# Expert weights of two routed layers: a load from DRAM per tile, or one resident copy in SBUF that each tile copies from

## The chip, the cores and the metric

The kernel runs on one core of a Trainium2 chip. The metric is the device time of one execution in microseconds. Thirteen executions of the kernel before have a median of 928.32 us, between 923.73 and 933.23.

## The reference

Four residual layers work on x of 16 batches x 128 tokens x 128 features, all fp32, each on the layer norm of x:

```python
x = x + xcond(layernorm(x), cond, ctx)      # self- and cross-attention, GLU
x = x + moe0(layernorm(x))                  # a shared expert and 7 routed ones
x = x + slots(cond, ctx, layernorm(x))      # 3 turns of slot attention
x = x + moe1(layernorm(x))                  # 8 routed experts

def moe0(x):                                # hidden width 352
    scores, idx = top_k(softmax(x @ wr.T + rb), 2)
    w = scores / scores.sum()
    out = expert(x, sg, su, sd)             # silu(x @ g.T) * (x @ u.T) @ d
    for e in range(7):
        out = out + w[e] * expert(x, rg[e], ru[e], rd[e])
    return out

def moe1(x):                                # hidden width 512
    probs = softmax(x @ w_gate + b_gate)
    e, p = argmax(probs), max(probs)
    return p * (relu(x @ W1[e] + b1[e]) @ W2[e] + b2[e])
```

A token goes to two of seven experts in the first routed layer and to one of eight in the second. Which ones is known only on the chip.

## The kernel before, in words

All tokens stay in SBUF in one tile, r (128 partitions x 16 batches x 128). The kernel goes through attention, the GLU (to some 495 us), the first routed layer, the slot attention and the second routed layer in that order, in groups of four batches.

A routed layer is an object of class `Routed`: m0 with two experts a token (nk = 2), m1 with one (nk = 1). Its work has four steps.

- **Routing.** Each group's normed rows go to DRAM (`rows`, the tensor tok, by SyncE's queue), with the token's weight beside them. DVE marks each token's experts.
- **Sorting** (`sort`). Every expert's tokens fill tiles of 128 rows; an expert's last tile may be partly empty. The number of tiles is a constant, the largest that can occur: (4096 + 7 x 127) // 128 = 38 for m0 and (2048 + 8 x 127) // 128 = 23 for m1. The sort, mostly small DVE operations, leaves for each tile the rows to fetch (frm), the rows to write (to), and in `row` the place of its expert's weights.
- **Tiles** (`tiles`). Each tile's 128 rows are fetched by an indirect DMA on POOL (L874, zs), transposed on TensorE and copied by ScalarE (L886, L888, zT). For m0, `moe0_up` (L978) makes two up-projections of 384 columns each into PSUM (gum). `silu_gate` makes th on ScalarE (L953), gs and a on VectorE (L955, L956). `moe0_down` (L989) projects back to 128 features (ynm) and ScalarE scales by the token's weight wk (L987, L993). An indirect DMA on POOL (L895) writes the rows to res in DRAM. For m1, `moe1_up` (L1231) makes two halves of the 512 hidden columns (h1n), with the relu on ScalarE (L1236) and VectorE (L1238). `moe1_down` (L1246) projects back, VectorE adds the bias and scales (L1248, L1249, ysn), and the rows go to the output.
- **Combine** (`combine`). For m0 the rows of res are read back per group (L925, ygm, eight loads on SyncE's queue) and added to r on TensorE (L921, L926) and ScalarE (L927). The slot attention's first turn waits for its group.

The loop over tiles is pipelined by its order of statements: the first half of tile j's up-projection, then the transpose of tile j + 1, then the second half, then the down-projection of tile j - 1 (`finish`), which also issues the weights of a later tile and the fetch of a later tile.

**Weights.** A tile's weights (gate, up and down side by side, 1152 columns for m0, 1156 with the biases for m1) come from DRAM by one DMA on SyncE's queue (L864). Its address is a register that SyncE loads from `row` (L861). Six buffers of 1156 columns let five loads go ahead of the tile at work. Only the first two are issued before the fetches: the later ones read their rows from `row_late`, a copy of `row` that is made to depend on the last steps of the sort.

**What sets the order.** Within an engine, instructions run in the order in which they are listed; a scheduler in the framework may move an instruction ahead of others while the kernel is built, except in a stretch marked as manual. Buffers of one tag in a pool come free in order, and a writer waits until the last reader of the old contents is done. So slot work that doesn't depend on the routed layer (`slot_prologue`, `slot_context`, L1031 to L1077) can stand between tiles or behind them, as the scheduler decides.

Of the kernel before, what the change touches and what calls it, by code (L numbers as in the profile page):

```python
# [11 lines left out]
F32 = mybir.dt.float32  # L12
BF16 = mybir.dt.bfloat16
I32 = mybir.dt.int32
# [17 lines left out]
WBUFS = 6  # L32
WT = 1156
# [24 lines left out]
def pixart_kernel(  # L58
# [577 lines left out]
    def wide(nm):  # L636
# [3 lines left out]
    wt = ctx.enter_context(tc.tile_pool(name="wt", bufs=WBUFS))  # L640
# [4 lines left out]
    cb = slp.tile([P, B, D], F32, name="cb")  # L645
    dma(
        out=cb,
        in_=rows[0, R_COND * D : (R_COND + B) * D].partition_broadcast(P).rearrange("p (b d) -> p b d", d=D),
    )


    def glu_body(g, hT):
        u = ph.tile([P, 4, 512], F32, name=f"u{g}", tag="act")
        for c in range(4):
            ps = {}
            for j in (1, 0):
                ps[j] = wide(f"glu{g}_{c}_{j}")
                PE.matmul(ps[j], lhsT=gluw[:, 4 * j + c, :], rhs=hT, start=True, stop=True)
            ge = ph.tile([P, 512], F32, name=f"ge{g}_{c}", tag="gate")
            S.activation(ge, ps[1], AF.Gelu, bias=col(C_FFB1 + 4 + c))  # L660
            V.scalar_tensor_tensor(u[:, c, :], ps[0], col(C_FFB1 + c), ge, ALU.add, ALU.mult)
        y = psX.tile([P, 4, D], F32, name=f"yg{g}", tag="x")
        token_major(y, lambda c: u[:, c, :], lambda c: gluw[:, 8 + c, :], 4)
        rg = r[:, 4 * g : 4 * g + 4, :]
        V.tensor_tensor(rg, y, rg, ALU.add)
# [38 lines left out]
    w_issue = []  # L704

# [5 lines left out]
    class Routed:  # L711


        def __init__(self, nm, ne, nk, w, w0, tok):
            self.nm, self.ne, self.nk, self.w, self.w0, self.tok = nm, ne, nk, w, w0, tok
            self.ws, self.zs, self.st = [], {}, {}
            self.b0, self.nb = 0, B
            nb = self.nb
            self.nt = n_tiles(nk * nb * P, ne)
            self.oh = self.tile([P, nk, nb, ne], "oh")  # L720
            self.any = self.tile([P, nb + 1, ne], "any")
            self.cum = self.tile([P, nb + 1, ne], "cum")
            V.memset(self.any[:, nb, :], 0.0)
            V.memset(self.cum[:, 0, :], 0.0)
# [32 lines left out]
        def sort(self):  # L757
# [27 lines left out]
            V.tensor_scalar(te, te, float(ne - 1), float(P), ALU.min, ALU.mult)  # L785
            V.tensor_scalar(self.row, te, float(self.w0), None, ALU.add)
# [52 lines left out]
            self.row_late = self.tile([1, nt], "row_late", I32)  # L839
            self.ahead = nk * (FETCH - 1)  # L840
            for _ in range(2):
                self.weights()
            for j in range(self.ahead):
                self.fetch(j)
            late = self.frm[:1] if nk == 2 else self.zs[0][:1, :nt].bitcast(I32)
            V.scalar_tensor_tensor(self.row_late, late, 0, self.row, ALU.mult, ALU.add)
            for _ in range(2, WBUFS - 1):
                self.weights()
# [5 lines left out]

        def weights(self):
            j = len(self.ws)
            if j == self.nt:
                return
            w = wt.tile([P, WT], F32, name=f"w{self.nm}{j}", tag="w")
            with tc.issue_after(w_issue[-1]) if w_issue else ExitStack():  # L860
                row = nc.sync.value_load(  # L861
                    (self.row if j < 2 else self.row_late)[0:1, j : j + 1], min_val=self.w0, max_val=self.w0 + (self.ne - 1) * P
                )
                w_issue.append(dma(out=w[:, : self.w.shape[1]], in_=self.w[bass.ds(row, P), :]).ins)  # L864
            self.ws.append(w)
# [13 lines left out]
        def tiles(self, up, down):  # L879

            nt, zs, zT, acts = self.nt, self.zs, {}, {}
            dst = res0 if self.nk == 2 else out.rearrange("b s d -> (b s) d")
            wrote = dram_disjoint_views(dst, nt)

            def turn(j, t):
                PE.transpose(t, zs[j][:, :D], ident)  # L886
                zT[j] = ph.tile([P, P], F32, name=f"zTn{self.nm}{j}", tag="zTn", bufs=3)
                S.copy(zT[j], t)  # L888

            def finish(j):  # L890
                y = ys4[:, 1 + j % 3, :]
                ys = ph.tile([P, D], F32, name=f"ys{self.nm}{j}", tag="ysn", bufs=6)
                down(self.ws[j], acts[j], y, ys, self, j)
                self.weights()
                G.indirect_dma_start(  # L895
                    out=wrote[j], out_offset=bass.IndirectOffsetOnAxis(ap=self.to[:, j : j + 1], axis=0),
                    in_=ys, in_offset=None, **({} if self.nk == 2 else dict(bounds_check=NTOK - 1, oob_is_err=False)),
                )
                self.fetch(j + self.ahead)


            ys4 = psX.tile([P, 4, D], F32, name=f"yn{self.nm}", tag="x")
            turn(0, ys4[:, 0, :])
            for j in range(nt + 1):
                steps = up(self.ws[j], zT[j], f"{self.nm}{j}") if j < nt else None
                if steps:
                    spare = next(steps)
                if j + 1 < nt:
                    turn(j + 1, spare)
                if steps:  # L910
                    acts[j] = next(steps)
                if j >= 1:
                    finish(j - 1)
# [44 lines left out]
    def moe0_shared(R, i, zT):  # L958
        g = R.b0 // 4 + i
        a = ph.tile([P, 3, 512], F32, name=f"ma{g}", tag="act")  # L960
        for c in range(3):
# [4 lines left out]
            silu_gate(a[:, c, :], ps[0], ps[1], f"s{g}_{c}", 512)  # L966
        y = psX.tile([P, 4, D], F32, name=f"ym{g}", tag="x")
        token_major(y, lambda c: a[:, c, :], lambda c: wsh[:, 2 * IP + c * D : 2 * IP + (c + 1) * D], 3)
# [48 lines left out]
    def work(g, nm, shape=(P, 512)):  # L1017

        return spool.tile(list(shape), F32, name=nm, tag=f"w{g}")

# [30 lines left out]
    def slot_prologue():  # L1051
        G.memset(vu[:, :, D : D + 1], 1.0)
        G.tensor_tensor(cb[:1], cb[:1], brow[:1, R_B2S, :].unsqueeze(1).to_broadcast([1, B, D]), ALU.add)
# [105 lines left out]
    def slot_mlp(it, g, hT):  # L1159
# [11 lines left out]
            yf, lhsT=ones[:1, :], rhs=cb[:1, 4 * g : 4 * g + 4, :].rearrange("p a d -> p (a d)"), start=True, stop=False  # L1171
# [52 lines left out]
    def moe1_up(w, zT, nm):  # L1224
        acts = []
        for j in range(2):
# [6 lines left out]
            for c in range(2):  # L1233
                src, b1 = ps[:, c * P : (c + 1) * P], 2 * M1 + 2 * j + c
# [9 lines left out]
    def moe1_down(w, a, y, ys, R, j):  # L1244
        for c in range(4):
            PE.matmul(y, lhsT=a[c], rhs=w[:, M1 + c * D : M1 + (c + 1) * D], start=(c == 0), stop=(c == 3))  # L1246
        z = R.zs[j]
        V.tensor_tensor(ys, y, w[:, 2 * M1 + 4 : 2 * M1 + 4 + D], ALU.add)  # L1248
        V.scalar_tensor_tensor(ys, ys, z[:, D : D + 1], z[:, D + 1 :], ALU.mult, ALU.add)  # L1249


    spool = ctx.enter_context(tc.tile_pool(name="sp", bufs=2))
# [36 lines left out]
    m1 = Routed("n", EX1, 1, moe1_w, 0, tok1)  # L1289
    zT = {}  # L1290
# [8 lines left out]
    m0.tiles(moe0_up, moe0_down)  # L1299
    slot_prologue()  # L1300
# [11 lines left out]
def _layout(a):  # L1312
# [33 lines left out]
    def wide(w):  # L1346
# [5 lines left out]
        cat([w1, chunks(w2), b1.reshape(-1, P).T, np.broadcast_to(b2, (P, D))], axis=1)  # L1352
# [38 lines left out]
```

## Time and profile before

| | |
|---|---|
| median of 13 executions | 928.32 us |
| profiled execution, its own time | 931.63 us |
| span of its trace | 929.7 us |
| mean granted TensorE clock | 0.945 |
| busy: TensorE, VectorE, ScalarE, POOL | 89%, 64%, 48%, 37% |
| moved by DMA | 61.82 MB |
| first up-projection of m0's tiles, last down-projection's end | 543.8, 648.2 us |
| first up-projection of m1's tiles, last down-projection's end | 850.1, 925.1 us |

A line of the groups names the source line, the engine, the operation, output and inputs by the program's names (buffer numbers left out), the shapes and the count, then busy us and the mean ns of one, then the idle time just before and what ended it. A line of the timeline gives start and duration in us, then engine, line, operation and count, and in brackets the idle time before it. A releaser is inferred from semaphore events. Names end in m for the first routed layer and in n for the second.

### The profile page before, as it was taken

The page shows a single profiled execution, that of the slowest core. Times are in us where ns is not written, and L with a number is a line of the kernel's source. Part 1 is how long each engine was busy: PE and PEld are TensorE (multiplying, and loading weights), DVE is VectorE, ACT ScalarE, POOL GpSimd, SP SyncE. Part 2 cuts the span into 40 slices and gives each one's busy share as a digit, 9 for nine tenths or more (in the row PEclk, how much of TensorE's full clock was granted, in tenths as well). Part 3 has the DMA queues.
Part 4 walks back from the last instruction along what each step waited for, and adds up shares of the span by engine and source line. Part 5 has one row for each costly group of instructions (what it writes and reads, how often), then busy time and mean ns, then how long its engine had stood idle before and what let it go on. Part 6 is the DMA issues. An engine that isn't in the chain of part 4 may idle for free.

```text
span 929.7 us, 16297 instructions
## 1 busy us (share of the span) xinstructions
PE 827.2 (89%) x5847; PEld 654.8 (70%) x5847; DVE 592.4 (64%) x1845; ACT 442.0 (48%) x950; POOL 346.5 (37%) x408
## 2 busy tenths in 40 slices
PE   6999999998999999999999788789858979967786
PEld 5688888877777877777665477779446756646675
DVE  4587776669566666668778634445477758764333
ACT  3666667665554444444222022334477677831222
POOL 2333333234232213224420446654433334423554
PEclk9999999999999999999999779999979979975989
DMA  8100000000000000002001437775300000026773
GB/s 323 54 2 1 1 2 2 1 1 1 2 1 1 2 1 2 1 2 73 1 23 48 154 94 240 244 244 186 91 1 1 1 1 1 24 49 219 232 228 107
DMA packets 29563, 61.82 MB, mean 66 GB/s; under 512 B 4266, under 2 KB 18045, under 8 KB 28843
## 3 DMA queue, kind: packets, MB, share of 16 engines
q1 hardware_dynamic: 25211, 51.70, 17.4%
q0 software_dynamic: 4272, 9.09, 3.2%
q8 instruction: 46, 0.75, 0.3%
q14 instruction: 34, 0.28, 0.1%
HBM read 54.01 MB, written 7.23 MB: 66 GB/s over the span
## 4 chain that ended last, share of the span: by engine, by line
PE 64%; DVE 19%; POOL 5%; ACT 4%; issue 3%; DMA 2%; another core or an unknown queue 2%; SPq 0%; POOLq 0%; ACTq 0%; DVEq 0%
PE gum L978 6%; PE po L441 6%; PE pv L339 6%; PE te L431 5%; PE ya L451 5%; PE s L380 4%; PE pk L332 3%; PE ynm L989 3%; PE pq L322 3%; PE s L389 3%; PE ynn L1246 3%; PE h1n L1231 2%; DVE ri L412 2%; DVE e L405 1%
## 5 line engine op out<-in xcount | busy, mean ns | idle before, releaser
L416 POOL TENSOR_TENSOR e<-e,ri 128x1024 f32<-128x1024 f32 (+1 forms) x64 | 100.6, 1573 | 250.8 <-DVE ri L413 207.3
L400 DVE TENSOR_REDUCE mx<-s 128x8 f32<-128x1024 f32 (+1 forms) x64 | 64.5, 1007 | 48.5 <-PE s L389 39.6
L412 DVE TENSOR_REDUCE ri<-e 128x8 f32<-128x1024 f32 (+1 forms) x64 | 64.2, 1003 | 27.2 <-ACT e L408 26.2
L432 ACT COPY eT<-te 128x512 f32<-128x512 f32 (+1 forms) x96 | 56.4, 587 | 51.0 <-PE te L431 50.4
L978 PE MATMUL gum<-zTnm,wm 128*128 128x128 f32 x456 | 65.5, 286 | 11.1 <-ACT zTnm L888 8.5
L431 PEld LDWEIGHTS te<-ident,e 128*128 128x128 f32 (+1 forms) x512 | 61.5, 144 | 19.6 <-issue 11.5
L431 PE MATMUL te<-ident,e 128*128 128x128 f32 (+1 forms) x512 | 74.8, 274 | 0.0
L322 PE MATMUL pq<-ha,wa 128*128 128x256 f32 x256 | 66.9, 398 | 3.8 <-DVE r L455 2.8
L441 PE MATMUL po<-eT,v 128*64 128x128 f32 (+1 forms) x1024 | 69.4, 277 | 0.0
L978 PEld LDWEIGHTS gum<-zTnm,wm 128*128 128x128 f32 x456 | 59.2, 199 | 13.6 <-ACT zTnm L888 9.7
L408 ACT ACTIVATE e<-e 128x1024 f32<-128x1024 f32 (+1 forms) x64 | 57.1, 892 | 23.1 <-DVE e L405 21.4
L441 PEld LDWEIGHTS po<-eT,v 128*64 128x64 f32 (+1 forms) x1024 | 58.0, 137 | 11.8 <-DVE eT L432 6.3
L405 DVE TENSOR_TENSOR e<-s,mx 128x1024 f32<-128x1024 f32 (+1 forms) x64 | 63.8, 997 | 2.0
L451 PEld LDWEIGHTS ya<-wa,oT 128*128 128x128 f32 x512 | 60.8, 192 | 3.9 <-issue 1.4
L451 PE MATMUL ya<-wa,oT 128*128 128x128 f32 x512 | 62.6, 275 | 0.0
L322 PEld LDWEIGHTS pq<-ha,wa 128*128 128x128 f32 x256 | 46.5, 198 | 12.2 <-DVE r L455 4.2
L874 POOL DMA_INDIRECT zsm<-tok,frmm x38 | 36.7, 967 | 43.7 <-DVE secm L852 21.6
L895 POOL DMA_INDIRECT res<-ysm,tom x38 | 37.3, 982 | 31.5 <-ACT ysm L993 18.2
L343 ACT COPY v<-pv 128x512 f32<-128x512 f32 (+1 forms) x64 | 37.3, 585 | 22.9 <-PE pv L339 22.9
L445 ACT COPY oT<-po 128x512 f32<-128x512 f32 x47 | 27.1, 576 | 42.8 <-PE po L441 42.8
L955 DVE SCALAR_TENSOR_TENSOR gsm<-thm,gum 128x384 f32<-128x384 f32 x38 | 21.1, 554 | 37.6 <-ACT thm L953 17.9
L380 PE MATMUL s<-k,ha 128*128 128x308 f32 x128 | 42.6, 436 | 0.0
(388 smaller groups left out, 1889.2 us busy)
## 6 DMA issues: line engine op xcount, KB each, us to landing
wm<-in_moe_w_dram SPq DMA_DIRECT2D x38, 576.0 KB
wn<-in_moe_w_dram SPq DMA_DIRECT2D x23, 578.0 KB
wa<-in_attn_w_dram SPq DMA_DIRECT2D x4, 1024.0 KB
ygm<-res SPq DMA_DIRECT2D x8, 256.0 KB
tok<-stm SPq DMA_DIRECT2D x4, 258.0 KB
tok<-stn SPq DMA_DIRECT2D x4, 258.0 KB
x<-in_x_dram SPq DMA_DIRECT2D x8, 128.0 KB
cb<-in_rows_dram SPq DMA_DIRECT2D x1, 1024.0 KB
```

The lines of the kernel that those rows point to most:

```text
L322: PE.matmul(pq[:, j, :], lhsT=wqk[:, w : w + P], rhs=hT, start=True, stop=True)
L380: PE.matmul(ps[:, par, : 4 * nk].rearrange("p (j k) -> p j k", k=nk), lhsT=st["qT"][:, i * P : (i + 1) * P], rhs=st["kT"][:, h0 : h0 + 4, ...
L400: V.tensor_reduce(self.mx, self.ps, AX.X, ALU.max)
L405: V.tensor_tensor(self.e, self.ps, self.mx.unsqueeze(3).to_broadcast([P, 2, 4, nk]), ALU.subtract)
L408: S.activation(self.e, self.e, AF.Exp, scale=1.0 / math.sqrt(DH))
L412: V.tensor_reduce(self.ri, self.e, AX.X, ALU.add)
L416: G.tensor_tensor(self.e, self.e, self.ri.unsqueeze(3).to_broadcast([P, 2, 4, self.nk]), ALU.mult)
L431: PE.transpose(t[:nk, j, :], e[:, par, j, :], ident)
L432: (copies or (S.copy, V.tensor_copy))[par](eT[:nk, par], t[:nk])
L441: PE.matmul(po[par * DH : (par + 1) * DH, j, :], lhsT=st["v"][:nk, i, 8 * hg + 2 * j + par, :], rhs=eT[:nk, par, j, :], start=True, stop=True,
L451: PE.matmul(y, lhsT=oT[:, c, :], rhs=st["wo"][:, 1024 + c * D : 1024 + (c + 1) * D], start=(c == 0), stop=(c == 7),)
L978: PE.matmul(ps[j][:, c * P : (c + 1) * P], lhsT=w[:, k : k + P], rhs=zT, start=True, stop=True)
```

## The change

The weights of all experts of a layer lie in SBUF in one tile, `wall`. It is loaded once per layer by `load()`, with one DMA for each expert on SyncE's queue (7 x 576 KB for m0, 8 x 578 KB for m1). m0's load is issued ahead of the GLU and the routing. m1's load goes into the same buffer, is issued behind m0's tiles and ahead of the slot attention, and so waits until the last tile of m0 has copied its weights.

Each tile still has its own weight tile, now three buffers instead of six. It is filled by two copies out of `wall`: the up part by VectorE (768 columns for m0, 644 for m1 with its biases) and the down part by ScalarE (384 and 512). Each of the two engines loads the address into a register of its own. Two tiles' copies are made in the sort, the others in `finish`. `row` now holds a column of `wall` and not a row of DRAM; `row_late` is gone.

The loop over tiles stands in a stretch of manual schedule, so that its instructions keep the order in which the kernel states them.

Room in SBUF is made in three places: the intermediate tiles of the GLU and of the shared expert take four tags of work tiles that the slot attention also uses; the work tiles move into the pool ph, and their old pool is gone; and the tile cb of condition rows, 16 rows wide on 128 partitions, becomes four rows wide with four groups of 32 partitions. m1's weights are laid out with the biases ahead of the second matrix.

The diff, cut to its core:

```diff
-WBUFS = 6
-WT = 1156
+WBUFS = 3
+UP0, DN0 = 768, 384
+UP1, DN1 = 644, 512
...
-    wt = ctx.enter_context(tc.tile_pool(name="wt", bufs=WBUFS))
+    wt = ctx.enter_context(tc.tile_pool(name="wt", bufs=1))
...
-    cb = slp.tile([P, B, D], F32, name="cb")
-    dma(
-        out=cb,
-        in_=rows[0, R_COND * D : (R_COND + B) * D].partition_broadcast(P).rearrange("p (b d) -> p b d", d=D),
-    )
-
+    cb = slp.tile([P, 4, D], F32, name="cb")
+    for g in range(4):
+        k = (R_COND + 4 * g) * D
+        dma(
+            out=cb[32 * g : 32 * g + 32],
+            in_=rows[0, k : k + 4 * D].partition_broadcast(32).rearrange("p (b d) -> p b d", d=D),
+        )
...
+    def work(g, nm, shape=(P, 512)):
+
+        return ph.tile(list(shape), F32, name=nm, tag=f"w{g}")
...
-        u = ph.tile([P, 4, 512], F32, name=f"u{g}", tag="act")
+        u = [work(c, f"u{g}_{c}") for c in range(4)]
...
-            self.nm, self.ne, self.nk, self.w, self.w0, self.tok = nm, ne, nk, w, w0, tok
-            self.ws, self.zs, self.st = [], {}, {}
+            self.nm, self.ne, self.nk, self.tok = nm, ne, nk, tok
+            self.zs, self.st, self.ws = {}, {}, []
+            self.up, self.dn = (UP0, DN0) if nk == 2 else (UP1, DN1)
+            self.w, self.w0, self.wn = w, w0, self.up + self.dn
...
-            V.tensor_scalar(te, te, float(ne - 1), float(P), ALU.min, ALU.mult)
-            V.tensor_scalar(self.row, te, float(self.w0), None, ALU.add)
+            V.tensor_scalar(self.row, te, float(ne - 1), float(self.wn), ALU.min, ALU.mult)
...
-            self.row_late = self.tile([1, nt], "row_late", I32)
             self.ahead = nk * (FETCH - 1)
-            for _ in range(2):
-                self.weights()
             for j in range(self.ahead):
                 self.fetch(j)
-            late = self.frm[:1] if nk == 2 else self.zs[0][:1, :nt].bitcast(I32)
-            V.scalar_tensor_tensor(self.row_late, late, 0, self.row, ALU.mult, ALU.add)
-            for _ in range(2, WBUFS - 1):
+            for _ in range(WBUFS - 1):
                 self.weights()
...
+        def load(self):
+
+            self.wall = wt.tile([P, EX1 * (UP1 + DN1)], F32, name=f"wall{self.nm}", tag="wall")
+            for e in range(self.ne):
+                dma(
+                    out=self.wall[:, e * self.wn : (e + 1) * self.wn],
+                    in_=self.w[self.w0 + e * P : self.w0 + (e + 1) * P, :],
+                )
+
         def weights(self):
+
             j = len(self.ws)
             if j == self.nt:
                 return
-            w = wt.tile([P, WT], F32, name=f"w{self.nm}{j}", tag="w")
-            with tc.issue_after(w_issue[-1]) if w_issue else ExitStack():
-                row = nc.sync.value_load(
-                    (self.row if j < 2 else self.row_late)[0:1, j : j + 1], min_val=self.w0, max_val=self.w0 + (self.ne - 1) * P
-                )
-                w_issue.append(dma(out=w[:, : self.w.shape[1]], in_=self.w[bass.ds(row, P), :]).ins)
+            w = wt.tile([P, UP1 + DN1], F32, name=f"w{self.nm}{j}", tag="w", bufs=WBUFS)
+            for eng, k, n, copy in ((V, 0, self.up, V.tensor_copy), (S, self.up, self.dn, S.copy)):
+                at = eng.value_load(self.row[0:1, j : j + 1], min_val=0, max_val=(self.ne - 1) * self.wn)
+                copy(w[:, k : k + n], self.wall[:, bass.ds(at + k, n)])
             self.ws.append(w)
...
-            ys4 = psX.tile([P, 4, D], F32, name=f"yn{self.nm}", tag="x")
-            turn(0, ys4[:, 0, :])
-            for j in range(nt + 1):
-                steps = up(self.ws[j], zT[j], f"{self.nm}{j}") if j < nt else None
-                if steps:
-                    spare = next(steps)
-                if j + 1 < nt:
-                    turn(j + 1, spare)
-                if steps:
-                    acts[j] = next(steps)
-                if j >= 1:
-                    finish(j - 1)
+            with tc.manual_schedule():
+                ys4 = psX.tile([P, 4, D], F32, name=f"yn{self.nm}", tag="x")
+                turn(0, ys4[:, 0, :])
+                for j in range(nt + 1):
+                    steps = up(self.ws[j], zT[j], f"{self.nm}{j}") if j < nt else None
+                    if steps:
+                        spare = next(steps)
+                    if j + 1 < nt:
+                        turn(j + 1, spare)
+                    if steps:
+                        acts[j] = next(steps)
+                    if j >= 1:
+                        finish(j - 1)
...
-        a = ph.tile([P, 3, 512], F32, name=f"ma{g}", tag="act")
+        a = [work(c, f"ma{g}_{c}") for c in range(3)]
...
-        G.tensor_tensor(cb[:1], cb[:1], brow[:1, R_B2S, :].unsqueeze(1).to_broadcast([1, B, D]), ALU.add)
+        row_add(cb, R_B2S, 4)
...
-            PE.matmul(y, lhsT=a[c], rhs=w[:, M1 + c * D : M1 + (c + 1) * D], start=(c == 0), stop=(c == 3))
+            PE.matmul(y, lhsT=a[c], rhs=w[:, UP1 + c * D : UP1 + (c + 1) * D], start=(c == 0), stop=(c == 3))
         z = R.zs[j]
-        V.tensor_tensor(ys, y, w[:, 2 * M1 + 4 : 2 * M1 + 4 + D], ALU.add)
+        V.tensor_tensor(ys, y, w[:, M1 + 4 : M1 + 4 + D], ALU.add)
...
-    spool = ctx.enter_context(tc.tile_pool(name="sp", bufs=2))
...
     m1 = Routed("n", EX1, 1, moe1_w, 0, tok1)
+    m0.load()
     zT = {}
...
     m0.tiles(moe0_up, moe0_down)
+    m1.load()
     slot_prologue()
```

More of the change, by code (lines that the diff above doesn't have):

```diff
@@ L660, in glu_body @@
             S.activation(ge, ps[1], AF.Gelu, bias=col(C_FFB1 + 4 + c))
-            V.scalar_tensor_tensor(u[:, c, :], ps[0], col(C_FFB1 + c), ge, ALU.add, ALU.mult)
+            V.scalar_tensor_tensor(u[c], ps[0], col(C_FFB1 + c), ge, ALU.add, ALU.mult)
         y = psX.tile([P, 4, D], F32, name=f"yg{g}", tag="x")
-        token_major(y, lambda c: u[:, c, :], lambda c: gluw[:, 8 + c, :], 4)
+        token_major(y, lambda c: u[c], lambda c: gluw[:, 8 + c, :], 4)
         rg = r[:, 4 * g : 4 * g + 4, :]
@@ L702, in pixart_kernel @@
     G.iota(jt, pattern=[[1, NTM]], base=0, channel_multiplier=0, allow_small_or_imprecise_dtypes=True)
-    w_issue = []
     batch_row = rt.tile([P, 2 * B], F32, name="batch_row")
@@ L965, in moe0_shared @@
                 PE.matmul(ps[j], lhsT=wsh[:, w : w + P], rhs=zT, start=True, stop=True)
-            silu_gate(a[:, c, :], ps[0], ps[1], f"s{g}_{c}", 512)
+            silu_gate(a[c], ps[0], ps[1], f"s{g}_{c}", 512)
         y = psX.tile([P, 4, D], F32, name=f"ym{g}", tag="x")
-        token_major(y, lambda c: a[:, c, :], lambda c: wsh[:, 2 * IP + c * D : 2 * IP + (c + 1) * D], 3)
+        token_major(y, lambda c: a[c], lambda c: wsh[:, 2 * IP + c * D : 2 * IP + (c + 1) * D], 3)
         rg = r[:, 4 * g : 4 * g + 4, :]
@@ L1015, in pixart_kernel @@
     vu0 = slp.tile([NC, D], F32, name="vu0")
-    def work(g, nm, shape=(P, 512)):
-        return spool.tile(list(shape), F32, name=nm, tag=f"w{g}")
     def slot_context(g):
@@ L1170, in slot_mlp @@
         PE.matmul(
-            yf, lhsT=ones[:1, :], rhs=cb[:1, 4 * g : 4 * g + 4, :].rearrange("p a d -> p (a d)"), start=True, stop=False
+            yf, lhsT=ones[32 * g : 32 * g + 1, :], rhs=cb[32 * g : 32 * g + 1].rearrange("p a d -> p (a d)"),
+            start=True, stop=False,
         )
@@ L1233, in moe1_up @@
             for c in range(2):
-                src, b1 = ps[:, c * P : (c + 1) * P], 2 * M1 + 2 * j + c
+                src, b1 = ps[:, c * P : (c + 1) * P], M1 + 2 * j + c
                 if j == 0:
@@ L1351, in _layout @@
     moe1 = [
-        cat([w1, chunks(w2), b1.reshape(-1, P).T, np.broadcast_to(b2, (P, D))], axis=1)
+        cat([w1, b1.reshape(-1, P).T, np.broadcast_to(b2, (P, D)), chunks(w2)], axis=1)
         for w1, w2, b1, b2 in zip(*[a["L1_ffn_" + n] for n in ("W1", "W2", "b1", "b2")])
```

## The prediction

> **What bounds the kernel now.** I read the counts, then the 40 slices (TensorE is busy nearly everywhere, the DMA engines only at the start and in two later stretches), then the chain of waits, then a table of windows over the two late stretches. Those are the two loops over routed tiles, the only place where the change touches much. The first loop (m0, 38 tiles) runs from its first up-projection at 543.8 us to its last down-projection at 648.2: 104.4 us, 2.75 us a tile. The second (m1, 23 tiles) runs from 850.1 to 925.1: 75 us, 3.26 us a tile. The windows give span, then busy time of PE, weight load, DVE, ACT and POOL, granted clock, DMA share and GB/s:
>
> ```profile
> 580.00:600.00 20.00, 14.89 (x119) 13.58 (x117) 8.03 (x18) 5.82 (x18) 12.72 (x13) 1.00 0.79 240
> 620.00:640.00 20.00, 20.00 (x180) 20.00 (x180) 12.40 (x30) 9.76 (x29) 9.31 (x10) 1.00 0.90 289
> 880.00:900.00 20.00, 13.88 (x90) 12.71 (x91) 6.72 (x22) 4.45 (x15) 11.04 (x12) 0.88 0.74 228
> ```
>
> The second row is the loop with nothing in its way: 180 matmuls in 20 us at full clock, 19 passes a tile, so 2.12 us. The first row is the same loop with its fetches and weight loads: PE idles a quarter of the time. The loads are these:
>
> ```profile
> wm<-in_moe_w_dram SPq DMA_DIRECT2D x38, 576.0 KB
> wn<-in_moe_w_dram SPq DMA_DIRECT2D x23, 578.0 KB
> ```
>
> So m0 loses 104.4 - 38 x 2.12 = 24 us to waits. Part is POOL: one row fetch (967 ns) and one row write (982 ns) a tile start 1.25 us apart when nothing else waits, 2.5 us a tile while both go on (26 of 38 tiles). Part is the traffic: the chain has several pieces of 2.5 us in these stages put down to "another core or an unknown queue", and one of 6.62 us at 535.6, ahead of the first tile.
>
> **What the change removes.** All 61 tile loads from DRAM (35 MB), with them their share in those unknown waits. The most that this can give m0 is the 24 us, and only if nothing slower stands in the loop.
>
> **What it adds to m0's loop.** The order of instructions in the changed kernel shows DVE's list of tile j as: gs(j), a(j), wk(j-1), a register load, then the copy of the 768 up columns of w(j+1). Two buffers of three are filled ahead, so tile j's step copies the weights that tile j+1's first matmul, next on PE after ynm(j-1), needs. That copy stands behind a(j), and a(j) behind both of tile j's up-projections. In the kernel before, a load ran several tiles ahead and no engine copied. So a new loop closes: gum(j), th(j), gs(j), a(j), wk, copy w(j+1), gum(j+1). Its pieces are in an iteration of before that started after a stall:
>
> ```profile
> 588.36 0.94 PE L978 MATMUL gum<-zTnm,wm 128*128 128x128 f32 x6 [1.18 <-ACT zTnm L888]
> ...
> 589.44 0.27 ACT L888 COPY zTnm<-gum 128x128 f32<-128x128 f32 x1 [0.48 <-issue]
> ...
> 589.61 0.50 ACT L953 ACTIVATE thm<-gum 128x384 f32<-128x384 f32 x1
> 589.87 0.27 DVE L987 TENSOR_SCALAR wk<-zsm,sgnm,secm 128x1 f32<-128x1 f32 x1
> ...
> 590.13 0.56 DVE L955 SCALAR_TENSOR_TENSOR gsm<-thm,gum 128x384 f32<-128x384 f32 x1
> ...
> 590.79 0.56 DVE L956 SCALAR_TENSOR_TENSOR am<-gsm,gum 128x384 f32<-128x384 f32 x1
> ```
>
> From gum's first matmul to th 1.25 (the next tile's transpose and its ACT copy go ahead of th, in both kernels), to gs 1.77, to a 2.43, a's end 2.99, plus wk 0.27: 3.26 us before the copy can start. The transfer of the instruction's result to PE costs some 0.05 (in these rows one engine starts 0.02 to 0.05 after the other's end).
>
> The copy itself: before has no DVE copy inside SBUF. Ends: not under 0.34, the 77x128 TENSOR_SCALAR of zc (336 ns), a sixth of the elements; not over 1.00, the 128x1024 reduction of e (L412, 1003 ns mean over both its sizes). I take 0.55, the duration of the loop's own DVE operations on 384 columns with two operands, since a copy has one operand and no PSUM in it. Period: 3.26 + 0.55 + 0.05 = 3.86 us, between 3.65 and 4.31. 38 tiles: 146.7 us, against 104.4: **+42 us** (+34 to +59). Of the old limits, PE (2.12) and POOL (2.5) fit under this period, so none of their waits is added; that is also why the removed traffic returns nothing here.
>
> The ACT copy (384 down columns, 0.5 by the 128x384 th row) stands behind ys(j-1), which ends some 2.6 us into the tile. It ends near 3.1 and is needed only by ynm(j+1): nothing. Cover gone, it would cost only what exceeds 3.8.
>
> The register load is unpriced. On SP, the load (270 ns median) and its register operations (152) take 0.65 us from the load's start to the DMA's issue (at 568.18), with SP otherwise idle. On DVE it has no operand of the loop, so the sequencer may do it while a(j) is still at work: 0 to 0.65 a tile, 0 to 25 us in m0, and the same step in m1 0 to 15. I take 0, as the back-to-back DVE rows start without a gap (gs to a: 0.66 with 0.56 busy), so dispatch runs ahead; the other end is a rival below.
>
> The Trainium skill, "VectorE: DVE Perf Modes", section "Mode 2×_2P — use both read ports for one tensor", has a one-source fp32 operation within SBUF at two elements a cycle. An estimate from its 0.96 GHz and its fixed 150 cycles is 0.56 us for 768 columns, the sum unchanged. Against the change, "SBUF — State Buffer", section "SBUF: two separate sides", says that such a copy locks GpSimd out of the shared port, so that it can't write DMA descriptors meanwhile. In before's trace the row fetches beside the zc operations at 534.5 took 0.95 us like the others. If every copy held POOL for its whole length, POOL would still be at 2.5 + 0.6 = 3.1 us a tile, under 3.86.
>
> **m1's loop.** There DVE's list is: the two relu operations of tile j, ysn(j-1) in two operations, register load, copy of 644 columns of w(j+1). ysn(j-1) waits for ynn(j-1), which PE runs after tile j's up-projection; h1n(j+1) waits for the copy. PE's 17 passes at 0.111 are 1.9 us at full clock, 2.15 at the 0.88 of the row above; then ysn 0.29 and 0.35, the copy 0.46 (0.34 to 0.84), hand-overs 0.15: 3.15 to 3.4. Now 3.26. I take **0** (-6 to +10).
>
> **Around the loops.** Each sort gets two copies with their register loads on DVE, ahead of work that leads to the fetches: +1.5 each, **+3** (1 to 5). The 6.62 us wait at 535.6 has no named cause; weights and fetches move at once there, and later only fetches do: between 0 and -6.6, I take **-3**. Slot-context pieces (L1045, L1047: 0.21 and 0.41) fall into m0's first tiles: 16 of them and a few more, mostly in DVE time after the copy that waits for PE: **+1**. They leave the tail, but it is not their wait that ends last there:
>
> ```profile
> L925 SPq EVENT_SEMAPHORE  x8: 17/28/9015, 638.6 to 662.7; - x8
> L925 SPq DMA_DIRECT2D ygm<-res x8: 359/371/506, 651.3 to 663.2; - x8
> ```
>
> Here SP sits 9.0 us until the last row write has landed, and the first matmul on a read-back (ygm) starts at 657.35. In the changed kernel the eight m1 loads (4.6 MB) stand ahead of ygm on SP's queue, and wait for the last copy out of the same buffer, some 5.5 us before the loop's end. At 289 GB/s they take 16 us, so ygm lands some 12 us after the loop's end instead of the 9 at which it is used now: **+3** (0 to +6). m0's weights load once at about 437 to 452, where the DMA engines idle and the next entry on SP's queue is a store at 464.7: nothing; late by 13 us, it would delay the routing rows. The smaller cb (256 KB for 1 MB), the shared tags and the moved biases: nothing, -1 to +1.
>
> **Sum.** 42 + 0 + 3 - 3 + 1 + 3 = +46 us. The profiled run took 931.63 us (span 929.7), 3.3 over the median of 928.32; on the median the sum is **974 us**, with its bounds 955 to 998.
>
> **Rivals.** *Register loads not hidden*: +25 in m0 and +15 in m1, 1014 us. For it: the copy's address comes from that register, on the same engine. Against it: it needs only a row that is ready long before. *A small loss, 940*: the copy at 0.34, m1 down to 2.6 us a tile without traffic (-15), the 6.62 gone, the tail hidden: 974 - 8 - 15 - 4 - 3 = 944, less 4 of the sorts and pieces. *Faster*: the copies lie under other work, because m0's next up-projection finds its weights ready. Its place is the hand-over from a(j) to gum(j+1), it decides once the period is under 2.75 us, and then POOL's 2.5 binds: 38 x 0.25 = -9.5 in m0, 23 x 0.76 = -17.5 in m1, with the head and tail as above 928 - 27 + 1 = 902. Against it stands DVE's order, under which a's end alone is at 2.99. *It does not do what it says* would be the same: 928, with the traffic gone but no wait ended by it, in which case gains and losses cancel.
>
> **Chances.** Forecast 0.52 (own range 955 to 998), register loads 0.22, small loss 0.10, faster 0.13, the same 0.03. A run of this kernel can tell about 0.3% (3 us) from no change. So faster 0.13, same 0.03, slower 0.84. The range leaves out the faster case and the top of the register case: 940 to 1020.
>
> **What would show it.** In m0, windows of 20 us would hold about 5.2 tiles (98 matmuls against 119), PE busy near 60%, and PE's idle before gum would be ended by DVE's copy of wm. POOL's fetches would no longer stand 1.25 us apart. The rows of the register load on DVE would show whether a gap stands between wk and the copy. In the tail, ygm would land after the last m1 load. I am wrong if gum's wait names zTnm again, if the copy is under 0.34 or over 1 us, or if the period of m0 is under 3.6.

## The result, and the profile after

The changed kernel takes 1053.99 us (median of 10 executions, 1049.95 to 1056.28) against 928.18 us (median of 46): a ratio of 1.1349, 95% interval 1.133 to 1.1368. The profiled execution took 1050.67 us, its span is 1049.0. The forecast was 974 us with a range of 940 to 1020: the direction was right, the size was not.

The time by stage, from the profiles, in us. A loop runs from its first up-projection to the end of its last down-projection; "between" is the slot attention with the second routing and sort. "Again" is a second profile of each kernel, both taken on one chip. "Forecast" gives the differences that the prediction adds up.

| profile | ahead of the first loop | first loop (a tile) | between | second loop (a tile) |
|---|---|---|---|---|
| before | 543.8 | 104.4 (2.75) | 201.9 | 74.9 (3.26) |
| after | 539.3 | 151.0 (3.97) | 206.2 | 147.8 (6.43) |
| difference | -4.5 | +46.6 | +4.3 | +72.9 |
| forecast | -1.5 | +43 | +4.5 | 0 |
| before, again (e5) | 542.8 | 106.7 (2.81) | 199.7 | 72.2 (3.14) |
| after, again (e6) | 541.5 | 149.0 (3.92) | 207.6 | 147.8 (6.43) |

Three of the four terms came out within 4 us. The fourth, the second loop, was put at no change and cost 73.

Windows of after, columns as in the prediction; the first row lies in the first loop, the other two in the second:

```profile
620.00:640.00 20.00, 11.80 (x98) 10.99 (x97) 9.27 (x20) 7.71 (x21) 9.95 (x11) 1.00 0.12 33
950.00:970.00 20.00, 12.54 (x53) 10.86 (x52) 5.09 (x16) 4.36 (x13) 5.98 (x6) 0.50 0.10 28
990.00:1010.00 20.00, 12.53 (x55) 11.00 (x55) 5.48 (x16) 4.94 (x13) 5.71 (x6) 0.59 0.07 20
```

In the first loop there are 98 matmuls where before had 119, at full clock, with the DMA engines at 0.12: what was forecast. In the second loop the granted clock is 0.50 to 0.59, and 53 matmuls go through in 20 us where before had 90 at 0.88. Both loops now wait for the same thing, by the groups of after (busy, mean ns, then the idle time ahead and its releaser):

```profile
L988 PE MATMUL gum<-zTnm,wm 128*128 128x128 f32 x456 | 65.7, 287 | 45.2 <-DVE wm L873 42.1
...
L1238 PE MATMUL h1n<-zTnn,wn 128*128 128x128 f32 x184 | 49.9, 427 | 37.6 <-DVE wn L873 37.3
```

The same groups of before, and the transposes of its second loop:

```profile
L978 PE MATMUL gum<-zTnm,wm 128*128 128x128 f32 x456 | 65.5, 286 | 11.1 <-ACT zTnm L888 8.5
...
L1231 PE MATMUL h1n<-zTnn,wn 128*128 128x128 f32 x184 | 31.1, 321 | 8.8 <-ACT zTnn L888 7.0 <-issue 1.8
...
L886 PE MATMUL h1n<-ident,zsn 128*128 128x128 f32 x22 | 7.6, 348 | 7.1 <-ACT an L1236 7.1
```

In after, VectorE's copy of the next tile's weights ends 42.1 us of idle time ahead of gum, and 37.3 ahead of h1n. In before, the waits of both were 11.1 and 8.8 us, most of it for ScalarE's copy of the transposed rows. The first loop's step on VectorE, from the timeline of after:

```profile
600.67 0.56 DVE L965 SCALAR_TENSOR_TENSOR gsm<-thm,gum 128x384 f32<-128x384 f32 x1 [1.89 <-ACT thm L963]
601.33 0.56 DVE L966 SCALAR_TENSOR_TENSOR am<-gsm,gum 128x384 f32<-128x384 f32 x1
601.80 0.27 DVE L997 TENSOR_SCALAR wk<-zsm,sgnm,secm 128x1 f32<-128x1 f32 x1
602.15 0.56 DVE L873 COPY wm<-wallm 128x768 f32 x1
```

gs, a, wk and the copy follow each other as in the forecast, and the copy takes 0.56 us where 0.55 was taken. The next gum starts at 602.86, the one after at 606.8: 3.93 a tile against 3.86.

The second loop, one tile of it, from the timeline of after (PE, DVE and ScalarE; weight loads and POOL left out):

```profile
966.72 1.19 PE L1238 MATMUL h1n<-zTnn,wn 128*128 128x128 f32 x4 [1.77 <-DVE wn L873]
...
967.95 0.63 ACT L1243 ACTIVATE an<-h1n,wn 128x128 f32<-128x128 f32 x2 [4.25 <-PE h1n L1238]
...
968.63 0.48 PE L895 MATMUL h1n<-ident,zsn 128*128 128x128 f32 x1 [0.72 <-ACT an L1243]
...
968.90 1.06 PE L1238 MATMUL h1n<-zTnn,wn 128*128 128x128 f32 x4
...
969.75 1.91 PE L1253 MATMUL ynn<-wn,an 128*128 128x128 f32 x8
...
971.70 0.29 DVE L1255 TENSOR_TENSOR ysn<-ynn,wn 128x128 f32<-128x128 f32 x1 [1.10 <-PE ynn L1253]
972.03 0.35 DVE L1256 SCALAR_TENSOR_TENSOR ysn<-ysn,zsn 128x128 f32<-128x128 f32 x1
...
972.80 0.50 DVE L873 COPY wn<-walln 128x644 f32 x1 [0.42 <-issue]
...
973.44 0.55 PE L1238 MATMUL h1n<-zTnn,wn 128*128 128x128 f32 x1 [1.78 <-DVE wn L873]
```

This is a closed chain of 6.72 us. Its order is the forecast's (up-projection, ynn, ysn, copy, next up-projection), but three things are in it that the forecast had not: PE waits 0.72 us for the relu before it transposes the next tile, VectorE waits 0.42 us ahead of the copy for nothing but its register, and the eight matmuls of ynn take 1.91 us (1.06 in e1 below, at full clock). The experiments price each.

### The profile page after: what moved, and what is told of

Read it like the earlier page. It is cut to its first block, busy times and chain, and to the rows that moved or that the text cites. A ratio compares the mean times of both kernels' runs of the same rounds, so it can differ in the third digit from the quotient of the medians.

```text
span 1049.0 us, 16434 instructions
## 1 busy us (share of the span) xinstructions
PE 860.0 (82%) x5847; PEld 678.8 (65%) x5847; DVE 621.6 (59%) x1902; ACT 473.3 (45%) x1009; POOL 344.4 (33%) x408
## 5 line engine op out<-in xcount | busy, mean ns | idle before, releaser
L988 PE MATMUL gum<-zTnm,wm 128*128 128x128 f32 x456 | 65.7, 287 | 45.2 <-DVE wm L873 42.1
L1238 PE MATMUL h1n<-zTnn,wn 128*128 128x128 f32 x184 | 49.9, 427 | 37.6 <-DVE wn L873 37.3
L1238 PEld LDWEIGHTS h1n<-zTnn,wn 128*128 128x128 f32 x184 | 43.6, 326 | 43.5 <-issue 42.8
L1245 DVE TENSOR_SCALAR an<-h1n,wn 128x128 f32<-128x128 f32 x46 | 14.0, 346 | 78.8 <-PE h1n L1238 78.8
L904 POOL DMA_INDIRECT out_dram<-ysn,ton x23 | 23.2, 1010 | 99.4 <-DVE ysn L1256 99.4
L1243 ACT ACTIVATE an<-h1n,wn 128x128 f32<-128x128 f32 x46 | 14.4, 364 | 90.6 <-PE h1n L1238 89.2
```

The source lines that it names most:

```text
L904: G.indirect_dma_start(out=wrote[j], out_offset=bass.IndirectOffsetOnAxis(ap=self.to[:, j : j + 1], axis=0), in_=ys, in_offset=None, **({} ...
L988: PE.matmul(ps[j][:, c * P : (c + 1) * P], lhsT=w[:, k : k + P], rhs=zT, start=True, stop=True)
L1238: PE.matmul(ps[:, c * P : (c + 1) * P], lhsT=w[:, k : k + P], rhs=zT, start=True, stop=True)
```

## The experiments

The theory after the result (A): the copies stand at the end of VectorE's list for a tile, which closes a loop through PE in both layers, and in the second the idle time that this leaves on PE lets the clock fall to half, so that the loop takes longer again. The rival (B): the copies and register loads are dear in themselves, by their own time or by holding up POOL, wherever they stand.

Each group of runs was made on one chip. In the group of e1 to e4 the kernel before took 885.8 us (7 runs), 42 less than elsewhere; why was not tried. The changed kernel itself was not run on that chip. These runs are therefore read by stages of their profiles and not by their ratio to before; where an edit touches one loop only, the other loop serves as the control. Loops of different groups are compared as well, since the second loop of the changed kernel took 147.8, 147.8 and 149.8 us in after, e6 and e4. The edits below are cut to their core, and some comments in them are added.

**e1, a busy PE in the second loop.**

```diff
                 down(self.ws[j], acts[j], y, ys, self, j)
+                for _ in range(5 if self.nk == 1 else 0):
+                    PE.matmul(ys4[:, 0, :], lhsT=ident, rhs=ident, start=True, stop=True)
```

> The changed kernel with five extra matmuls (ident by ident into an unused part of PSUM) behind each down-projection of the second layer's tile loop; nothing else is changed. In the changed kernel this loop runs at a granted clock of 0.50 to 0.59 and 6.72 us a tile. Theory A (the copy that stands behind ysn closes a loop through PE, and the half clock doubles PE's share of it): the extra matmuls fall into PE's wait for the copy and raise the clock to 0.9 or more; the 17 passes cost 1.9 instead of 3.7 us a tile, the loop comes to 4.6 to 5.0 us a tile, the whole to 1010 to 1020 us. Theory B (register loads, copies and POOL's descriptors hold the period, the low clock is only a consequence): the period stays within 0.2 us of 6.72, the whole within 5 us of 1054 or above it.

The trace records each of these matmuls as two passes, so PE has 27 passes a tile instead of 17. The second loop took 111.8 us, 4.86 a tile, instead of 147.8; the first was unchanged (148.9). The whole was 1008.63 us. Windows of e1, at the start and in the middle of the second loop:

```profile
890.00:900.00 10.00, 7.79 (x32) 6.92 (x33) 2.36 (x7) 2.67 (x8) 3.72 (x5) 0.50 0.21 58
940.00:960.00 20.00, 14.97 (x109) 12.77 (x108) 7.00 (x20) 6.61 (x18) 8.60 (x9) 1.00 0.13 40
```

The clock goes from 0.50 to 1.00. Added work made the loop 36 us shorter, so half clock accounts for about half of the 73 us, the largest single part: A.

**e2, no register loads.**

```diff
-                at = eng.value_load(self.row[0:1, j : j + 1], min_val=0, max_val=(self.ne - 1) * self.wn)
-                copy(w[:, k : k + n], self.wall[:, bass.ds(at + k, n)])
+                copy(w[:, k : k + n], self.wall[:, k : k + n])
```

> The changed kernel with the copies taken from a constant place, so that no engine loads a register in the tile loops. It leaves out the choice of the expert: every tile uses the first one. Theory A (register loads are a small, measured gap of 0.42 us before the copy in the second loop and some 0.1 to 0.15 in the first): -10 us in the second loop, -4 to -6 in the first, the whole at 1036 to 1042 us. Theory B (the register loads are the price that the forecast left out): -40 us or more, below 1015 us. If the loads are hidden altogether: within 3 us of 1054.

The second loop took 133.2 us (5.79 a tile, 0.64 less than after's 6.43), the first 142.2 (3.74, 0.18 less than e1 on the same chip). The whole took 1016.29 us, lower than A expected and 1.3 above B's bound. The loads cost 14.6 us in the second loop (16.6 against e4 below, which has the same loop on the same chip: 149.8) and 6.7 in the first: more than A had said and less than B's 40. The two sorts come out 5 us shorter than in e1, but the stage ahead of the first loop alone differs by 3.5 us between e1 and e3, which are equal there. The timelines of e1 and e2 show where the time goes, in the second loop:

```profile
952.47 0.35 DVE L1258 SCALAR_TENSOR_TENSOR ysn<-ysn,zsn 128x128 f32<-128x128 f32 x1
...
953.23 0.49 DVE L873 COPY wn<-walln 128x644 f32 x1 [0.41 <-issue]
```

```profile
946.83 0.35 DVE L1255 SCALAR_TENSOR_TENSOR ysn<-ysn,zsn 128x128 f32<-128x128 f32 x1
947.10 0.49 DVE L872 COPY wn<-walln 128x644 f32<-128x644 f32 x1
```

With the load the copy starts 0.76 us after ysn's second operation, without it 0.27: 0.49 us a tile, in e1 at full clock and in after (0.77) at half. The rest of e2's 0.64 goes with the clock: taken in stretches of 10 us, the second loop of e2 was granted more than 0.50 in 8 of 14, that of after in 3 of 15. In the first loop the copy starts 0.16 us earlier without the load (medians), since there most of the load lies under a and wk.

**e3, the copy at the head of the iteration, and e4, the same in the first loop alone.**

```diff
                 for j in range(nt + 1):
+                    if j:
+                        self.weights(both=False)      # VectorE's copy of w(j + 1)
                     steps = up(self.ws[j], zT[j], f"{self.nm}{j}") if j < nt else None
...
                 down(self.ws[j], acts[j], y, ys, self, j)
-                self.weights()
+                self.downs()                          # ScalarE's copy
```

> The changed kernel with one edit in the order: VectorE's copy of the up part stands at the head of the iteration, ahead of the operations of tile j, and not behind them; ScalarE's copy stays where it was. Same instructions, same buffers. Theory A (the place of the copy in VectorE's list closes the loop): the first loop falls from 3.93 to 2.3 to 2.8 us a tile (87 to 106 us), the second from 6.43 to 2.7 to 3.3 at a clock of 0.8 or more (62 to 76 us), the whole to 895 to 930 us. Theory B (the copies themselves cost: port, POOL's descriptors, register loads): the first loop stays over 3.1 us a tile and the second over 5, the whole over 980 us.

> As the early copy, but in the first layer's loop alone; the second layer's loop is as in the changed kernel. Theory A: the first loop as in the early copy, the second as in the changed kernel, so 1054 less some 50 us: 995 to 1010 us, and the two loops' gains add up. Theory B: over 1030 us.

e3: first loop 125.1 us (3.29), second 68.3 (2.97), clock 1.00 there from 880 us on, the whole 947.63. e4: 125.2 and 149.8 (6.51), the whole 1025.57. The same copies and loads, moved by a few instructions, cost the second loop 81 us less than in e4: B is out for it. The two gains add up: the whole differs by 1025.57 - 947.63 = 78 us, the second loop by 81.5. The first loop gained 24 us and not 50, so it stayed in B's range (over 3.1), and e4 lies over its expectation. What was late next there, from the timeline of e3:

```profile
600.81 0.50 ACT L980 ACTIVATE thm<-gum 128x384 f32<-128x384 f32 x1
...
601.34 0.55 DVE L982 SCALAR_TENSOR_TENSOR gsm<-thm,gum 128x384 f32<-128x384 f32 x1 [1.21 <-ACT thm L980]
...
602.00 0.55 DVE L983 SCALAR_TENSOR_TENSOR am<-gsm,gum 128x384 f32<-128x384 f32 x1
602.47 0.27 DVE L1014 TENSOR_SCALAR wk<-zsm,sgnm,secm 128x1 f32<-128x1 f32 x1
...
602.82 0.37 ACT L1020 ACTIVATE ysm<-ynm,wk 128x128 f32<-128x128 f32 x1 [1.51 <-PE gum L907]
...
603.50 0.51 ACT L880 COPY wm<-wallm 128x384 f32 x1 [0.31 <-issue]
603.91 0.26 ACT L909 COPY zTnm<-gum 128x128 f32<-128x128 f32 x1
604.07 0.49 ACT L980 ACTIVATE thm<-gum 128x384 f32<-128x384 f32 x1
```

A second closed chain of 3.26 us, from th to th: wk stands behind a on VectorE, ys waits for wk, and ScalarE's copy with its register load stands between ys and the next zT and th. In before the scheduler had put wk ahead of gs, at 589.87 in the prediction's lines; the order given by the kernel puts it behind a.

**e5 and e6, both kernels again on one chip.**

> The kernel before, unchanged, on the chip of this group of runs, for its stages. In the first group of experiments it took 885.8 us and not 928: a chip on which something is faster. Theory A (its tile loops wait for the weight loads, and the chip serves them faster): on a chip at 886 us the first loop takes 85 to 92 us instead of 104.4 and the second 52 to 62 instead of 75, the rest within 6 us of the profile of before. Theory B (another stage is faster): the loops stay within 5 us. On a chip at 928 us the stages repeat within 4 us.

> The changed kernel, unchanged, on the same chip. Its loops load no weights from DRAM. Theory A: its stages hardly depend on the chip, the loops 148 to 152 and 145 to 150 us, the whole 1040 to 1056 us, so that the ratio to the kernel before is 1.17 to 1.19 where before takes 886 us, and 1.13 where it takes 928.

This chip served before at 928.07 us (931.41 as median of the 13 runs beside it), so the question of e5 stays open. e6 took 1050.78 us, ratio 1.127 (1.1211 to 1.1329). The stages are in the table above: the loops of after repeat within 2 us.

**e7, wk worked out with the transpose.** To e3 is added:

```diff
             def turn(j, t):
+                if self.nk == 2:
+                    V.tensor_scalar(self.wk[j], zs[j][:, D : D + 1], ...)
...
-        V.tensor_scalar(wk, R.zs[j][:, D : D + 1], ...)
+        wk = R.wk[j]
```

> As the early copy (e3), with one more step moved in the first layer's loop: wk, the scale of a tile's rows, is worked out with the tile's transpose and no longer behind a(j) on VectorE. In e3 the loop th, gs, a, wk, ys, ScalarE's copy, next zT, next th took 3.26 us a tile. Theory A (that loop is what is late next, since ys waits for wk): the first loop falls from 3.30 to 2.5 to 2.8 us a tile (95 to 106 us), the second stays at 2.98 (66 to 70 us). Theory B (POOL is held by the copies, 2 x 0.97 plus 0.56 plus gaps): over 3.1 us a tile still.

First loop 113.0 us (2.97), the whole 943.02, on another chip than e3. The chain through wk was worth 12 us, so B is out for the first loop too, but the loop stops short of 2.8. The second loop took 75.6, more than in e3, though nothing in it was changed: it ran at half clock for its first 18 us, in e3 for 9.

**e8, three more moves.** To e7 are added: ScalarE's copy ahead of ys; in `moe1_up` the yield of the spare columns ahead of the relu; and the second layer's loads behind the read-back:

```diff
                     if j >= 1:
+                        self.downs()
                         finish(j - 1)
...
+            if j == 0:
+                yield spare
             for c in range(2):
...
-    m1.load()
     slot_prologue()
     slot_turns(range(4), m0.combine)
+    m1.load(m0.back)                  # issued after the last ygm load
```

> e7 with three more moves: ScalarE's copy stands ahead of ys and behind th; in the second layer the next tile's transpose is issued ahead of the relu that reads the same PSUM bank (0.72 us of PE's wait a tile in e3); the second layer's weights are loaded behind the read-back of res on SyncE's queue. Theory A: first loop 2.3 to 2.6 us a tile (88 to 99 us), second loop 2.0 to 2.5 (46 to 58 us), the stretch between the loops 3 to 5 us shorter, the whole 885 to 910 us: under 928 where before takes that, level with it where before takes 886. Theory B (a resident copy can't keep up with the loads): over 930 us.

935.64 us, ratio to before 1.0044 (1.0018 to 1.007): nearly level, not under it, and in the range of B. First loop 113.1 us, second 70.8 (3.08), between 203.8, which is 4.3 less than in e7. Windows of e8 in the first loop, with fetches and when they are over:

```profile
580.00:590.00 10.00, 8.38 (x70) 7.91 (x69) 6.67 (x15) 4.66 (x14) 6.53 (x8) 1.00 0.14 42
640.00:650.00 10.00, 10.00 (x89) 9.86 (x88) 8.35 (x21) 6.87 (x18) 4.33 (x5) 1.00 0.08 29
```

Without fetches PE is busy all the time; with them it idles a sixth of it, though no weights move. So the weight loads from DRAM are not what holds this loop, and moving ScalarE's copy gained it nothing. POOL's fetch and write a tile, some 2.6 us, fit the picture, but no run tests them; so do waits of some 2 us that hit VectorE and ScalarE at once four times in this loop (565.7, 589.7 among them). What ends these waits was not found.

**e9, a push at the start only.** As e1, with eight matmuls in the first four tiles (the expectation says three; the edit, and the 64 extra passes in the trace, make it four).

> The changed kernel with eight extra matmuls behind the down-projection in the first three tiles of the second loop alone (e1 had five in every tile). Theory A1 (the clock has two states that keep themselves: at full clock the loop's 17 passes in 4.9 us hold it, as the 19 passes in 3.93 us do in the first loop): the clock stays at 1.0 after the push, the second loop takes 112 to 120 us. Theory A2 (the clock follows the busy share, and 17 passes a tile are too few at any clock): it falls back to 0.5 within some 10 us, the loop takes 143 to 150 us.

```profile
900.00:910.00 10.00, 7.78 (x31) 6.60 (x32) 2.09 (x7) 2.66 (x8) 3.77 (x5) 0.50 0.25 66
910.00:920.00 10.00, 8.18 (x64) 7.42 (x62) 2.63 (x8) 3.01 (x8) 3.63 (x4) 0.96 0.14 38
920.00:930.00 10.00, 7.81 (x63) 7.24 (x64) 3.22 (x10) 2.52 (x8) 3.97 (x4) 1.00 0.13 39
930.00:940.00 10.00, 5.03 (x28) 4.12 (x27) 3.17 (x10) 2.63 (x7) 3.98 (x4) 0.73 0.08 23
940.00:960.00 20.00, 12.53 (x52) 10.85 (x51) 5.25 (x15) 4.52 (x12) 5.97 (x6) 0.50 0.09 27
```

Windows of e9: the push, whose last matmul is over at 927.7, lifts the clock to 1.00, and it falls back to 0.50 by 940. The loop took 141.5 us, a little under A2's range. The next tile, at full clock, takes 4.76 us (h1n at 927.53 and at 932.29). Seventeen passes of 0.111 us in that time, 40% of it, don't hold the clock; the first loop's 19 passes in 3.93 us, 54%, hold 1.00 from 560 to 680 us. So the slow clock is a consequence of the closed chain, and not left over from the sort.

**e10, e1 and e2 together.**

> e1 and e2 together: extra matmuls in every tile of the second loop, and copies from a constant place (it leaves out the choice of the expert; every tile uses the first one). Theory: at full clock a register load costs what it costs at half clock, 0.6 us a tile, since it stands on VectorE between ysn and the copy: second loop 4.86 - 0.62 = 4.2 to 4.3 us a tile, 97 to 100 us. If the loads' price was a part of the slow clock only: 4.7 or more.

The second loop took 106.8 us, 4.64 a tile, not 4.2. The timeline shows why: the five extra matmuls start at 952.45 and end past the copy (952.70 + 0.49); h1n follows at 953.67. The probe itself had become the bound, so the period says only that the load costs at least 0.22 us at full clock. The copy's start says more: 0.27 us after ysn's second operation (952.43), where e1 has 0.76, so 0.49 at full clock too.

**e11, the transpose ahead of the relu, with e1.** The edit is the `yield spare` of e8.

> e1 with the next tile's transpose ahead of the relu of the first half, in the second loop. In e1 PE waits for that relu before the transpose, and the forecast left this wait out. Theory: 0.6 to 0.8 us a tile, second loop 4.0 to 4.3 us a tile, 93 to 99 us. If the wait lies beside another on the path: within 0.1 us of 4.86.

89.7 us, 3.90 a tile: 0.96 less than e1, more than expected. The wait for the relu was on the path with its hand-overs. What is left of the chain, from the timeline of e11:

```profile
949.79 0.68 PE L1240 MATMUL h1n<-zTnn,wn 128*128 128x128 f32 x4
...
951.96 0.29 DVE L1257 TENSOR_TENSOR ysn<-ynn,wn 128x128 f32<-128x128 f32 x1 [0.28 <-PE ynn L1255]
952.29 0.35 DVE L1258 SCALAR_TENSOR_TENSOR ysn<-ysn,zsn 128x128 f32<-128x128 f32 x1
...
953.05 0.50 DVE L873 COPY wn<-walln 128x644 f32 x1 [0.41 <-issue]
...
953.70 0.68 PE L1240 MATMUL h1n<-zTnn,wn 128*128 128x128 f32 x4
```

**e12, e8 with two extra matmuls a tile in the second loop.**

> e8 with two extra matmuls behind each down-projection of the second loop, which ran at a clock of 0.83 to 1.0 there. Theory A (what is left of the second loop over 2.5 us a tile is clock): second loop from 3.08 to 2.5 to 2.8 us a tile, the whole 6 to 13 us under e8, and so 0.2 to 0.9% under the kernel before on the same chip. Theory B (POOL's two DMAs a tile, 2.6 us, and the waits of 2 us that hit several engines at once hold it): within 3 us of e8.

933.73 us, ratio 1.0077 (1.0054 to 1.01); the clock is 1.00 in the second loop from 861 us on, and the loop took 71.4 us all the same. What is left of it over 2.5 us a tile is not the clock. That is as B said, but what does hold it was not found. No version found beats the kernel before.

## Why the prediction was wrong

**The first loop was right**, by its own steps. "Period: 3.26 + 0.55 + 0.05 = 3.86 us" against 3.93; +46.6 us against +42, with +1 for the slot pieces. In after's rows the copy starts 3.22 us after gum, lasts 0.56, and the next gum starts 0.15 after its end. The 0.05 for that last step was read from rows in which other engines follow each other, none of them PE behind VectorE. The Trainium skill's estimate for the copy ("VectorE: DVE Perf Modes", section "Mode 2×_2P — use both read ports for one tensor"), 0.56 us, is the measured 560 ns. The lock of its page "SBUF — State Buffer", section "SBUF: two separate sides", shows at most faintly: in after's second loop 21 of POOL's 23 writes run beside a copy and take 1012 ns, against 1005 for these writes in before; in its first loop two of 38 do, with 1102 and 1122 ns against a mean of 984 for the others. No write was held for a copy's whole length.

**Around the loops the sums came out**: -4.5 us ahead (forecast -1.5), +4.3 between (+4.5). The stage ahead runs from 539.3 to 542.5 us in four profiles that have the same code there (after, e6, e9, e11), so its single terms are not shown. That the second layer's loads delay ygm is shown: the first matmul on ygm starts 12.5 us after the first loop's end in after and 5.7 after it in e8, which moves the loads and saves 4.3 us against e7.

**The step that failed is m1's loop: "Now 3.26. I take 0 (-6 to +10)."** The chain was named in the right order, as 3.15 us at full clock. It measured 6.72 in a tile at half clock and 6.43 over the loop:

- **The wait behind PE.** The 17 passes were taken as 1.9 us, with 0.15 for all hand-overs. From h1n's start to ysn's is 2.17 us in e11: +0.27. A pass of ynn lasts 275 ns there from start to end, though the next one starts 0.111 us after it, and VectorE waits for the end of the last one.
- **The register load** was put at 0, "so dispatch runs ahead". It does so only in part. In e1 the load's sequence begins at 952.49, just after ysn's second operation has started, and the copy starts at 953.23, so that 0.33 us of it is hidden and 0.41 bare. In the first loop a and wk hide all but 0.08. (The 0.65 us that the prediction read on SyncE is short as well: from the load to the DMA's issue it is 0.73 us or more in every row of before.)
- These two with some rounding give e11's 3.90 = 3.15 + 0.27 + 0.41 + 0.07.
- **The wait for the relu** was not in the sum at all: the next transpose goes into the PSUM tile that the relu reads. It stood in before's profile as an idle time of 7.1 us, ahead of 5 of the 22 transposes; in the closed chain every tile pays it: +0.96 (e1 against e11).
- **The clock** was carried over from before's row (0.88). The chain leaves PE at 39% of full-clock time, and the clock falls to half: +1.86 in a tile (6.72 against 4.86), 36 us over the loop.

The rival for this, register loads not hidden, was priced at +15 us in the second loop, close to e2's 14.6, and at +25 in the first, where e2 gave 6.7; it was given 0.22 and held alone. The clock was in no rival. The range's upper end had no case in which a longer period slows PE itself. Even without such a case its bounds, 955 and 998, are narrower than the ends of its terms added up, some 951 and 1010.

## What to carry to other kernels

Ask of each copy or load that feeds the next iteration where it stands in its engine's list: behind the work of the same iteration, it closes a loop of all engines, and its length is the sum of their steps. When such a loop is priced, work out the share of time that PE will be busy in it, because the clock that the sum assumes may not be granted; here 54% held full clock and 40% did not. The share of a whole loop is only a first hint: in e8's second loop, 17 passes in 3.08 us, 61%, the clock still fell to 0.66 (window 905 to 910) after a wait of 2.2 us on PE that began at 903.9. An order given by hand also freezes what the scheduler had done quietly, such as wk ahead of gs.

## What the runs showed of the hardware

- A register load on VectorE (median 303 ns; 0.74 us until the copy starts) began in both loops 0.02 to 0.06 us after the start of the last operation ahead of it that had itself to wait for another: ysn's second in e1 (952.47), a in after (601.33), with wk listed between a and the load. It left 0.41 us bare in the second loop and 0.08 in the first. On ScalarE the visible part was 0.3 us (603.50 in e3).
- The Trainium skill, "TensorE: Matmul & The Clock Gate", section "HAM oscillation — how this bites in real kernels", puts the fall of the clock down to idle gaps of more than some 3.4 us. In e9 the clock fell in a loop whose longest gap on PE was 1.78 us, while after's first loop held 1.00 through gaps of 1.92 us. So no single gap decided here; the two loops differ in PE's share (40% and 54%), but no run tests at which share the clock falls.
- A DVE copy of 768 fp32 columns within SBUF takes 560 ns and of 644 columns 497; ScalarE's of 384 and 512 take 512 and 618.
